# Turns given to other places in a four-layer graph network: block ends behind the third block, and layer 3's small steps

## The chip, the core and the metric

The kernel runs on one core of one Trainium2 chip. A core has five engines that each work through their own list of instructions in order: PE (matrix products), DVE (vector), ACT (scalar functions), POOL (GpSimd) and SP (here: DMA issue). The metric is the device time of one execution in microseconds (us); the kernel before takes 2223.41 us (median of 3 runs, 2222.41 to 2224.99).

## The reference

The input is x (4096 nodes with 128 features) and one sparse adjacency matrix adj (4096 x 4096, kept dense, f32). Four graph layers follow one another, each as `x = layernorm(x + layer(x, adj))`:

```
layer 0:  scores from signs of adj, softmax over edges, h' = (attn * adj) @ (x @ W)
layer 1:  two Chebyshev convolutions (K = 3), each with ELU:
          T1 = adj @ x ; T2 = 2 adj @ T1 - x ; out = x W[0] + T1 W[1] + T2 W[2] + b
layer 2:  4 heads: h = x @ weight.T ; C = src + dst
          tau = adj.T * exp(max(0.2 C, C)) ; z = sum over m of (adj.T * tau / sum tau) h, plus bias
layer 3:  deg = clip(sum adj, 1) ; out = x W_self + (adj @ x / deg) W_neigh
```

The output is x after layer 3.

## The kernel before, in words

The 4096 nodes are 32 tiles of 128 (index `t` or `nt`), and 8 blocks of 512 (`ib` or `b`). The matrix [...] streams in as pieces of 1 MB (`chunk`), again for each product.

**Where the change acts.** Everything from L1035 on is one hand-ordered stretch (`manual_schedule`): on PE, DVE, ACT and POOL the instructions run in the order in which the program emits them. Three kinds of work are woven into one another there:

1. Layer 1's last product (L1118): for each of the eight column blocks, 32 matmuls of w with pieces of the transposed matrix, summed in PSUM. Its accumulator p is emptied by the first instruction of `block_end` (L749).
2. Layer 2's attention. It is done in passes (class `Pass`): passes 0 to 5 are wide (two blocks of 512, two heads each), passes 6 and 7 narrow (one block, four heads). A pass has 32 steps, one for each source tile. In a step DVE makes tau (L880), DVE and POOL multiply it once more with the matrix (L886 to L888; narrow: L892 to L894), and PE sums numerator and denominator over the steps with four matmuls each (L904). ACT copies the piece of the matrix to PSUM (`a`, L852 or L849) and takes the row sums for layer 3's degree along with it.
3. Layer 3's product (`layer3_product`, L991): for each pair of blocks, 64 matmuls of 512 columns, and every column block is then added to acc3 (L998 by ACT for the first pair, L1000 by DVE for the others).

**Places.** Small dependent jobs are Python generators in a queue `chains`. Each `one(chains)` in the main order is a place: it runs the first generator up to its next `yield`. When a generator ends, the next one in the queue starts in the same place. So a `yield` is a gap: whatever stands between two yields is emitted together, and what comes after the yield is emitted behind the matmuls and steps up to the next place. The chains in question:

- `block_end(ib)` (L741): ELU, transposes, residual and layer norm of layer 1's block, transposes of x, then x @ W2S in two halves (L784) and from each half the exponentials cs and es and the weighted features hc (L791 to L796). A step of pass 0 or 1 for a source tile may be emitted only after the block's end is done.
- `block_targets(ib)` (L800): the target side of the scores, dv, one matmul (L804) and a string of copies and subtractions in PSUM (L806 to L813).
- `Pass.targets` (L855): a matmul with selD for each of the pass's four parts and ACT's copy to D.
- `Pass.finish` (L913): transposes of the denominator, reciprocal rd, transposes of the numerator, product z, and POOL adds z to x.
- `layer3_blocks(blocks)` (L937): per block, transposes of x, ACT's copy to xb, four layer-norm statistics on DVE (bn_stats and bn_aggr, lines L142 and L143) and 1/sqrt, then xb @ W3 in two halves (L957), which ACT scales into y and x (L966, L970). Only then `start_product` puts layer 3's product of these blocks into the queue `pieces`.

**How many places there are.** In column blocks 0 to 2 there is a place behind every second matmul (16 per column block). From column block 3 on, a column block is cut into groups by `cuts`: four groups for block 3, six for 4 and 5, five for 6 and 7. Each group has two steps, two places (in its middle and at its end) and then `products()`, PE's sums of earlier steps. Behind layer 1 the loop `while todo` makes rounds of two steps: step, place, step, a further place if no piece of layer 3 is waiting, `products()`, place, and then some layer-3 matmuls: a credit of 2.0 per wide round and 3.4 per narrow round, at most 6, which is set to zero while `pieces` is empty. A round stops handing out matmuls when a column block of layer 3 is complete; its addition to acc3 is emitted after the first step of the next round. What is left when the passes are done is emitted behind them.

Most of the chains' PSUM results go through one pool, ps_x, whose tiles are all named px, with one buffer: a new px waits until the last reader of the one before is done.

Of the kernel before, what the change touches and what calls it, by code (L numbers as in the profile page):

```python
# [33 lines left out]
def adj_resnorm_d4(ctx: ExitStack, tc: tile.TileContext, x_in, xT_in, adj, adjT, w0g, w0gT, a0, w1a, b1a,  # L34
# [10 lines left out]
    NB = N // IB  # L45
# [87 lines left out]
    def transpose4(pool, name, src, order=lambda r: r):  # L133

        p = pool.tile([P, TB, P], F32, name=name)
        for k in range(TB):
            order(nc.tensor.transpose(p[:, k, :], src(k), ident))  # L137
        return p

    def stats(r, t):  # L140
        st = small.tile([P, 6], F32, name="st")
        nc.vector.bn_stats(st, r)  # L142
        nc.vector.bn_aggr(mv[:, t, :], st)  # L143
# [481 lines left out]
    def network(usual):  # L625

        with ExitStack() as whole:
# [113 lines left out]
            def block_end(ib, p):  # L741

                blk = slice(ib * IB, (ib + 1) * IB)
                tb = slice(ib * TB, (ib + 1) * TB)
                pns = []
                oT = l2w.tile([P, IB], F32, name="oT", tag="z")
                rn = l2w.tile([P, 2, IB], F32, name="rn", tag="nd")
                r, n = rn[:, 0, :], rn[:, 1, :]
                nc.vector.tensor_add(oT, p, h0T[:, blk])  # L749
                nc.vector.tensor_scalar(n, oT, B1B, 0.0, op0=ALU.add, op1=ALU.min)  # L750
                nc.scalar.activation(n, n, AF.Exp)
                nc.scalar.activation(r, oT, AF.Relu, bias=B1B)
                nc.vector.scalar_tensor_tensor(oT, n, -1.0, r, op0=ALU.add, op1=ALU.add)
                yield
                if ib <= 2:
                    yield
                q = transpose4(ps_x, "px", lambda k: oT[:, k * P:(k + 1) * P])
                yield
                nc.vector.tensor_add(x[:, tb, :], q, x[:, tb, :])
                for t in range(ib * TB, (ib + 1) * TB):  # L760
                    stats(x[:, t, :], t)
                s = small.tile([P, TB], F32, name="rstd")
                m = small.tile([P, TB], F32, name="mean")
                nc.scalar.activation(s, mv[:, tb, 1], AF.Sqrt, bias=eps)
                nc.vector.reciprocal(s, s)
                nc.vector.scalar_tensor_tensor(m, mv[:, tb, 0], -1.0, s, op0=ALU.mult, op1=ALU.mult)
                for k in range(TB):
                    r = x[:, ib * TB + k, :]
                    nc.scalar.activation(r, r, AF.Identity, bias=m[:, k:k + 1], scale=s[:, k:k + 1])
                yield  # L770
                q = transpose4(ps_x, "px", lambda k: x[:, ib * TB + k, :])
                yield
                nc.scalar.copy(xT[:, blk], q.rearrange("p k i -> p (k i)"))
                nc.scalar.activation(m[:, 0:1], m[:, 0:1], AF.Exp, scale=0.0)
                nc.gpsimd.tensor_tensor(x[:, tb, :], x[:, tb, :], B2R[:, None, :].to_broadcast([P, TB, F]), ALU.add)  # L775
                if ib < NB - 2:
                    yield
                for half in range(2):

                    pool, name = (ps_p, "pp") if ib == NB - 1 and half else (ps_x, "px")  # L780
                    pn = pool.tile([P, 2, F + H], F32, name=name)
                    for k in range(2):
                        t = ib * TB + 2 * half + k
                        nc.tensor.matmul(pn[:, k, :], xT[:, t * P:(t + 1) * P], W2S, start=True, stop=True)  # L784
                    pns.append(pn)
                    if ib == NB - 1 and half == 0:
                        continue
                    yield
                    for pn, at in zip(pns, range(half + 1 - len(pns), half + 1)):
                        two = slice(ib * TB + 2 * at, ib * TB + 2 * at + 2)  # L790
                        nc.scalar.activation(cs[:, two, :], pn[:, :, F:F + H], AF.Exp, scale=0.2)  # L791
                        nc.scalar.activation(es[:, two, :], pn[:, :, F:F + H], AF.Exp, scale=0.8)
                        for k in range(2):
                            t = ib * TB + 2 * at + k
                            nc.vector.tensor_mul(hc[:, t], pn[:, k, 0:F].rearrange("p (h f) -> p h f", f=FO),
                                                 cs[:, t, :][:, :, None].to_broadcast([P, H, FO]))  # L796
                    pns.clear()
                ended.append(ib)

            def block_targets(ib):  # L800

                blk = slice(ib * IB, (ib + 1) * IB)
                pd = ps_x.tile([96, IB], F32, name="px")
                nc.tensor.matmul(pd, WD, xT[:, blk], start=True, stop=True)  # L804
                yield
                nc.scalar.activation(pd, pd, AF.Exp, scale=-0.8)  # L806
                nc.scalar.copy(dv[:, blk], pd)
                yield
                nc.vector.tensor_sub(pd, pd, dv[:, blk])
                nc.scalar.copy(dv[32:64, blk], pd[32:64, :])  # L810
                nc.scalar.copy(dv[64:96, blk], pd[64:96, :])
                nc.vector.tensor_sub(pd[64:96, :], pd[64:96, :], dv[64:96, blk])
                nc.scalar.copy(dv[64:96, blk], pd[64:96, :])  # L813
                if ib < 2:
                    yield
# [4 lines left out]
            class Pass:  # L820
# [92 lines left out]
                def finish(self):  # L913


                    more = (ps_p, "pp") if self in passes[0:2] else (ps_nd, "den") if self is passes[-1] else None
                    turn = lambda pool, name, i: transpose4(pool, name, lambda k: self.nd[:, i, k * P:(k + 1) * P])
                    q = turn(ps_x, "px", 1)
                    if more:
                        qn = turn(*more, 0)  # L920
                    yield
                    rd = small.tile([P, TB, 4], F32, name="rd")
                    nc.vector.reciprocal(rd, q.rearrange("p k (g f) -> p k g f", f=FO)[:, :, :, 0])
                    if not more:
                        qn = turn(ps_x, "px", 0)
                        yield
                    z = l2w.tile([P, TB, 4, FO], F32, name="z")
                    nc.vector.tensor_mul(z.rearrange("p k q f -> p (k q) f"), qn.rearrange("p k (g f) -> p (k g) f", f=FO),
                                         rd.rearrange("p k g -> p (k g)")[:, :, None].to_broadcast([P, TB * 4, FO]))
                    n, f = len(self.blocks), slice(self.heads[0] * FO, (self.heads[-1] + 1) * FO)  # L930
                    for i, b in enumerate(self.blocks):
                        xb = x[:, b * TB:(b + 1) * TB, f].rearrange("p k (h f) -> p k h f", f=FO)
                        eng = nc.vector if self is passes[-1] else nc.gpsimd
                        eng.tensor_tensor(xb, z.rearrange("p k (h b) f -> p k h b f", b=n)[:, :, :, i, :], xb, ALU.add)
                    yield

            def layer3_blocks(blocks):  # L937
# [3 lines left out]
                for j, b in enumerate(blocks):  # L941
# [7 lines left out]
                    nc.scalar.activation(sj, mv[:, b * TB:(b + 1) * TB, 1], AF.Sqrt, bias=eps)  # L949
                    nc.vector.reciprocal(sj, sj)  # L950
                    final = b == NB - 1
                    qs = []
                    for half in range(2):
                        pool, name = ((ps_nd, "den") if final else (ps_p, "pp") if blocks[0] == 0 else (ps_x, "px"))
# [81 lines left out]
            with tc.manual_schedule(engines={mybir.EngineType.PE, mybir.EngineType.DVE, mybir.EngineType.Activation,  # L1036
# [6 lines left out]
                passes = [Pass([2 * mp, 2 * mp + 1], [2 * hp, 2 * hp + 1]) for mp in range(NW - 1) for hp in range(H // 2)]  # L1043
# [33 lines left out]
                def num(this, nt, tau2):  # L1077
                    this.product(False, nt, tau2)
                    if nt == NT - 1 and this is not passes[-1]:
                        if this is passes[0]:  # L1080
                            first_sums.close()
                            ps_a.append(enter(name="ps_a2", bufs=1, space=PSUM))
                        chains.append(this.finish())
                        if this.heads[-1] == H - 1:
                            chains.append(layer3_blocks(this.blocks))
                            chains.append(start_product(this.blocks))
                            if this is passes[1]:
                                chains.append(block_targets(NB - 1))
                        later = passes.index(this) + 2
                        if 2 < later < len(passes):  # L1090
                            chains.append(passes[later].targets())
# [119 lines left out]
```

## Time and profile before

| row of the page | value |
|---|---|
| span | 2221.7 us, 23001 instructions |
| PE busy | 2136.2 us (96%) |
| DVE busy | 1186.1 us (53%) |
| ACT busy | 562.8 us (25%) |
| POOL busy | 857.5 us (39%) |
| L1118, PE, product with w | 203.1 us in the group of pp, 29.1 us in the group of num |
| L904, PE, numerator and denominator | 333.6 us and 339.2 us |
| L991, PE, layer 3's product | 231.7 us |
| L880, DVE, tau | 646.7 us, mean 1059 ns |
| L888, POOL, second factor | 459.4 us, mean 2393 ns |

The profile is that of one execution. Its page divides the span into 40 equal slices and gives each engine's busy share of a slice in tenths. A row of a group names line, engine, operation, output and inputs, then the time that the group was busy, the mean of one instruction and the idle time of the engine just ahead of it, with what ended that idle time. A view of waits sums such idle time by waiting line and by the line that ended it (total, times, longest). A view in order of time gives start, length and instruction, and idle time ahead of it in brackets. An f32 matmul appears there as two records.

### The profile page before, as it was taken

Reading aid. Unit: us, or ns where it says so; the run is one execution under the profiler, and the core shown is the slowest. Engines: PE = TensorE matmul, PEld = TensorE weight load, DVE = VectorE, ACT = ScalarE, POOL = GpSimd, SP = SyncE. Lnnn points to the kernel's source line nnn. Section 1 sums busy time; section 2 is a strip of 40 time slices with the busy share of each in tenths; the row PEclk is TensorE's granted clock in tenths of the full one; section 3 lists DMA queues with packets and bytes.
Section 4 is the critical chain, followed back from the end, with each engine's and each line's share of the span. In section 5 each row is a group of like instructions: output and inputs, shape, how many; then the busy total and the mean of one; then the engine's idle time right before and its main releaser. Section 6 shows DMA issues by size and latency. Waiting matters only on the chain. (4 is left out here: it accounts for less than half of the span.)

```text
span 2221.7 us, 23001 instructions
## 1 busy us (share of the span) xinstructions
PE 2136.2 (96%) x8644; PEld 847.9 (38%) x8644; DVE 1186.1 (53%) x1832; ACT 562.8 (25%) x1014; POOL 857.5 (39%) x539
## 2 busy tenths in 40 slices
PE   8999999999999999999999999979999899999997
PEld 4344454444444444444443333322222222223333
DVE  5655460000011110000016787799999999989995
ACT  6755100000000000000032323235333433232213
POOL 0000000000000000000005676698999899989980
PEclk9999999999999999999999999999999999999999
DMA  9886658888767677777876556525666566635554
GB/s 395 328 324 234 224 201 286 300 302 302 265 229 262 233 240 267 263 263 267 285 256 236 186 195 224 209 79 191 242 230 244 190 243 231 228 132 191 189 174 169
DMA packets 87145, 528.18 MB, mean 238 GB/s; under 512 B 9328, under 2 KB 15472, under 8 KB 25712
## 3 DMA queue, kind: packets, MB, share of 16 engines
q1 hardware_dynamic: 80288, 521.64, 66.6%
q10 hardware_dynamic: 6736, 4.98, 0.7%
q8 instruction: 70, 1.15, 0.2%
q14 instruction: 51, 0.42, 0.1%
HBM read 524.49 MB, written 2.10 MB: 237 GB/s over the span
## 5 line engine op out<-in xcount | busy, mean ns | idle before, releaser
L880 DVE SCALAR_TENSOR_TENSOR tau<-D,es,a 128x1024 f32<-128x1024 f32 (+1 forms) x640 | 646.7, 1059 | 45.9 <-ACT a L852 20.0
L888 POOL TENSOR_TENSOR tau<-tau,chunk 128x1024 f32<-128x1024 f32 x192 | 459.4, 2393 | 13.3 <-DVE tau L880 12.5
L775 POOL TENSOR_TENSOR x<-x,B2R 128x512 f32<-128x512 f32 x8 | 10.2, 1276 | 1145.0 <-PE px L137 1145.0
L904 PE MATMUL num<-tau,hc 128*32 128x512 f32 x2048 | 333.6, 613 | 15.5 <-POOL tau L888 9.1
L904 PE MATMUL den<-tau,cs 128*32 128x512 f32 x2048 | 339.2, 602 | 1.9 <-DVE tau L880 0.4
L991 PE MATMUL pp<-chunk,xT 128*128 128x512 f32 (+1 forms) x488 | 231.7, 604 | 0.0
L852 ACT ACTIVATE a<-chunk 128x1024 f32<-128x1024 f32 x160 | 164.4, 1027 | 253.7 <-DVE tau L886 193.1
L664 PE MATMUL pacc<-chunk,t 128*128 128x512 f32 x512 | 223.5, 592 | 0.0
L664 PE MATMUL pacc<-chunk,v 128*128 128x512 f32 x512 | 222.5, 592 | 0.0
L664 PE MATMUL pacc<-chunk,x 128*128 128x512 f32 x512 | 222.1, 592 | 0.0
L887 POOL TENSOR_TENSOR tau<-tau,chunk 128x320 f32<-128x320 f32 x192 | 168.0, 875 | 127.5 <-DVE tau L880 84.9
L1118 PE MATMUL pp<-chunk,w 128*128 128x512 f32 x448 | 203.1, 598 | 0.8 <-DVE oT L749 0.8
L379 PE MATMUL pacc<-chunk,hw 128*128 128x512 f32 x408 | 187.9, 605 | 0.8 <-DVE hw L421 0.7
L886 DVE TENSOR_TENSOR tau<-tau,a 128x704 f32<-128x704 f32 x186 | 163.4, 879 | 0.0
L894 POOL TENSOR_TENSOR tau<-tau,chunk 128x1024 f32<-128x1024 f32 x64 | 151.8, 2372 | 1.1
L904 PEld LDWEIGHTS num<-tau,hc 128*32 128x32 f32 x2048 | 61.5, 110 | 231.8 <-issue 129.6
L904 PEld LDWEIGHTS den<-tau,cs 128*32 128x32 f32 x2048 | 79.2, 111 | 173.8 <-issue 97.3
L664 PEld LDWEIGHTS pacc<-chunk,v 128*128 128x128 f32 x512 | 97.2, 190 | 122.0 <-issue 122.0
L664 PEld LDWEIGHTS pacc<-chunk,x 128*128 128x128 f32 x512 | 96.3, 190 | 115.8 <-issue 115.8
L664 PEld LDWEIGHTS pacc<-chunk,t 128*128 128x128 f32 x512 | 96.1, 190 | 115.3 <-issue 115.3
L991 PEld LDWEIGHTS pp<-chunk,xT 128*128 128x128 f32 x488 | 85.7, 189 | 128.6 <-issue 125.8
L711 DVE COPY w<-ptr 128x512 f32<-128x512 f32 x8 | 5.5, 692 | 241.5 <-PE ptr L137 241.5
(243 smaller groups left out, 1688.4 us busy)
## 6 DMA issues: line engine op xcount, KB each, us to landing
chunk<-in_adjT SPq DMA_DIRECT2D x386, 1024.0 KB, 4.9
chunk<-in_adj SPq DMA_DIRECT2D x80, 1024.0 KB, 5.0
chunk<-in_adj SPq DMA_DIRECT2D x32, 512.0 KB, 4.7
keep<-in_adjT SPq DMA_DIRECT2D x13, 1024.0 KB, 11.4
xT<-in_xT ACTq DMA_DIRECT2D x8, 256.0 KB, 6.6
out<-o ACTq DMA_DIRECT2D x7, 256.0 KB, 2.3
W1A<-in_w1a ACTq DMA_DIRECT2D x1, 384.0 KB, 6.8
W1B<-in_w1b ACTq DMA_DIRECT2D x1, 384.0 KB, 7.5
```

Of the source, the lines that this page charges most:

```text
L379: in_order(nc.tensor.matmul(p, hw[:, j * TB + k, :], a[:, k, :], start=first and k == 0, stop=last and k == TB - 1))
L664: nc.tensor.matmul(p, stationary(c * TB + k), a[:, k, :], start=n == 0 and k == 0, stop=n == NB - 1 and k == TB - 1)
L775: nc.gpsimd.tensor_tensor(x[:, tb, :], x[:, tb, :], B2R[:, None, :].to_broadcast([P, TB, F]), ALU.add)
L852: nc.scalar.activation(ap, a, AF.Copy, accum_out=deg[:, nt, self.mp:self.mp + 1])
L880: nc.vector.scalar_tensor_tensor(flat(tau[:, q:q + n]), flat(self.D[:, q:q + n]), es[:, nt, head:head + 1], ap, op0=ALU.max, op1=ALU.mult)
L886: nc.vector.tensor_tensor(t2[:, 0:OWN], t[:, 0:OWN], (a if only else ap)[:, 0:OWN], ALU.mult)
L887: nc.gpsimd.tensor_tensor(t2[:, OWN:WB], t[:, OWN:WB], a[:, OWN:WB], ALU.mult)
L888: nc.gpsimd.tensor_tensor(t2[:, WB:2 * WB], t[:, WB:2 * WB], a, ALU.mult)
L894: nc.gpsimd.tensor_tensor(tau2[:, 2:4, :], tau[:, 2:4, :], rep(a, 2), ALU.mult)
L904: nc.tensor.matmul(acc[32 * q:32 * q + 32, :], weights(nt, head, is_den), r[:, q, :], start=nt == 0, stop=nt == NT - 1)
L991: nc.tensor.matmul(p, y[:, c * TB + k, :], a[:, k, lo:lo + n], start=c == blocks[0] and k == 0, stop=end)
L1118: nc.tensor.matmul(p, w[:, c * TB + k, :], a[:, k, :], start=c == 0 and k == 0, stop=c == NB - 1 and k == TB - 1)
```

## The change

Six edits, all of them yields. Nothing else differs; every engine does the same work, in partly other order.

- `block_end`, block 2: one place less ahead of its first transposes, and one less between the copy of xT and x @ W2S.
- `block_end`, blocks 3 and 4: a place between the first half of W2S (its exponentials and hc) and the second.
- `block_targets`, blocks 3 to 6: a place between the block's end and the targets' matmul.
- `finish`, passes 2 to 6: a place between the pass's last products and its transposes.
- `layer3_blocks`, all blocks but the last: a place between the copy of x and the statistics on one side and the products with W3 on the other.

The purpose is that the producer of a transpose or a product is further ahead of it in the queue, and that each block's end and targets lie within the column block that follows.

```diff
-                if ib <= 2:
+                if ib < 2:
                     yield
                 q = transpose4(ps_x, "px", lambda k: oT[:, k * P:(k + 1) * P])
...
-                if ib < NB - 2:
+                if ib < NB - 2 and ib != 2:
                     yield
                 for half in range(2):
 
                     pool, name = (ps_p, "pp") if ib == NB - 1 and half else (ps_x, "px")
+                    if half and ib in (3, 4):
+                        yield
                     pn = pool.tile([P, 2, F + H], F32, name=name)
...
             def block_targets(ib):
 
                 blk = slice(ib * IB, (ib + 1) * IB)
+                if 2 < ib < NB - 1:
+                    yield
                 pd = ps_x.tile([96, IB], F32, name="px")
...
+                    if self in passes[2:-1]:
+                        yield
                     q = turn(ps_x, "px", 1)
...
                     final = b == NB - 1
+                    if not final:
+                        yield
                     qs = []
```

## The prediction

> **What bounds the kernel now.** I read the page first, then who waited for whom on PE, then the order of time of one wait after another, and last the starts of DVE's L880, which mark the rounds. The change begins to act after 1170 us, in the product with w (L1118), so the page is read from slice 22 on.
>
> ```profile
> PE   8999999999999999999999999979999899999997
> DVE  5655460000011110000016787799999999989995
> POOL 0000000000000000000005676698999899989980
> ```
>
> Slices are 55.5 us. From 1170 to 1440 us PE is full while DVE and POOL have room: PE sets the pace. From 1500 us DVE and POOL are full as well. There PE's nines deceive: a wide round (two steps) starts every 6.36 us, and its 16 accumulating matmul groups (4 x 0.86 us) and two L991 matmuls (0.89 us each) need 5.2 us. DVE needs 2 x 3.18 us (L880 starts at 1551.9, 1555.2 and so on), POOL 2 x (0.87 + 2.37) less overlap. So wide rounds are bound by DVE and POOL. Narrow rounds take 6.60 us with DVE, POOL and PE close together.
>
> ```profile
> PE px L137 <- ACT dv L813: 5.4, 1, 5.4
> PE px L957 <- ACT xb L945: 4.3, 4, 2.2
> PE px L804 <- DVE hc L795: 0.9, 1, 0.9
> ```
>
> These are PE's waits that the edits touch (total, times, longest). Only the first and third lie in the stage that PE bounds. The first, in order of time on PE:
>
> ```profile
> 1216.93 3.70 PE L1118 MATMUL pp<-chunk,w 128*128 128x512 f32 x8
> 1226.02 1.12 PE L137 MATMUL px<-ident,oT 128*128 128x128 f32 x4 [5.39 <-ACT dv L813]
> 1227.07 1.94 PE L904 MATMUL num<-tau,hc 128*32 128x512 f32 x8
> ```
>
> Block 3's transposes share a place with the last part of block 2's targets: px has one buffer, and PE stands until ACT's last copy out of it (L813). What that costs is read from the spacing of L749 on DVE, once per column block:
>
> ```profile
> 1212.61 0.69 DVE L749 TENSOR_TENSOR oT<-pp,xT 128x512 f32<-128x512 f32 x1 [2.67 <-PE pp L1118]
> 1273.57 0.69 DVE L749 TENSOR_TENSOR oT<-pp,xT 128x512 f32<-128x512 f32 x1 [1.63 <-PE pp L1118]
> 1330.89 0.69 DVE L749 TENSOR_TENSOR oT<-pp,xT 128x512 f32<-128x512 f32 x1
> ```
>
> Column blocks 4 and 5 hold the same matmuls and the same six groups: 60.96 and 57.32 us. In the second PE waits 0.65 us for the normalized x (L769), 0.60 for POOL and 0.32 for hc.
>
> In the layer-3 part I take the round of blocks 2 and 3 (DVE, idle time in brackets):
>
> ```profile
> 1727.11 0.26 DVE L142 BATCH_NORM_STATS2 st<-x 128x6 f32<-128x128 f32 x1
> 1727.41 0.18 DVE L143 BATCH_NORM_AGGREGATE mv<-st 128x2 f32<-128x6 f32 x1
> 1730.12 0.18 DVE L950 RECIPROCAL rstd<-rstd 128x4 f32<-128x4 f32 x1 [2.53 <-ACT rstd L949]
> 1730.21 2.44 DVE L880 SCALAR_TENSOR_TENSOR tau<-D,es,a 128x1024 f32<-128x1024 f32 x2
> ```
>
> DVE stands 2.53 us because ACT's square root is queued behind the copy of xb, an `a` load and the copy of a finished layer-3 column block (L998 at 1726.37). The whole cost of a boundary is its rounds' excess over 6.36 us: 4.29 and 3.15 here (10.65 and 9.51 us).
>
> **What the skill says.** Trainium Architecture — The Big Picture, "Inside one NeuronCore": every engine has its own stream, and they meet only at semaphores. The trace agrees: the 5.39 us are PE's, while DVE went on until its own queue needed PE. PSUM — Partial Sum Buffer, "Specifications (TRN2)": 8 banks of 2 KiB per partition; a px of 512 f32 is one whole bank, which fits the single buffer seen in the waits. ScalarE: Activation LUTs, "What ACT_TABLE_LOAD costs": 1283 ns for the load; the trace has 1.28 us, at 1728.49, inside the 2.53 us. TensorE: Matmul & The Clock Gate, Part 1, says that idleness slows the array; here the accumulating group right after the 5.39 us took 1.94 us against 1.06 usually, so a little more than the wait itself may come back.
>
> **Layer 1's last product.** I counted the places by the code. Two edits take one place each from block 2. Its end and targets then fill exactly the 8 places of column block 3 instead of running 2 places into column block 4. Block 3's transposes get the first place there, as block 4's have in column block 5. So column block 4 should look like column block 5: 60.96 - 57.32 = 3.64 us saved, the new waits of 0.65 and 0.60 included. The second W2S half of blocks 3 and 4 gets its own place, which removes the 0.32 us wait for hc. The target matmul of block 6 (L804) gets its own place too: 0.88. Sum: **-4.8 us**. New placing costs nothing elsewhere: block 2's transposes come after four L1118 matmuls (3.55 us) while oT is ready 2.5 us after the stage starts; its x transposes come after a group of products (2.6) and four more matmuls, as block 6's have now without a wait; copying xT and the first W2S half share a place, again as in block 6. Target copies of blocks 4 to 6 go one to two places later, still within places that are empty now. The waiting engine would be PE, with L1118 behind it. Bounds: -6.6 (5.39 + 0.32 + 0.88, nothing new) to -3.0 (block 2 also gets block 4's 1.25, and a little more).
>
> **Blocks 0 and 1 of layer 3.** The same DVE work, two statistics of some 2.2 us (1.6 plus 0.36 of ACT plus 0.18), now falls in two rounds instead of one; the sum is the same. PE loses its 0.74 and 2.96 us waits, which PE's slack hides. Copying out block 7's targets and the first selD share a place as before, but after products: PE can wait some 3.3 us there against 2.11 now, and arrive later at the next column block's end. **+0.5**, bounds -1.3 to +1.5.
>
> **Blocks 2 and 3.** The statistics no longer stand in the round that begins with the L998 copy ahead of them, but at its end. That round: 6.36 + 1.04 (what L998 costs in an ordinary round: 7.40 us) + 2.25 = 9.65; the next 6.36; the third 8.6. Sum 24.6 against 10.65 + 9.51 + 6.37 = 26.5: **-1.9**, bounds -2.5 to 0. The extra place ahead of the `finish` transposes moves rd and z by half a round; the wait of 0.65 us there is PE's and hidden.
>
> **Blocks 4 and 5.** Rounds 70 to 74 now exceed 6.60 us by 9.44 in sum. After: two accumulations of 0.6 and perhaps 0.4 of waiting, rd and z 0.8, statistics 4.5, one late `a` load 1.2: 7.9. That is -1.5, and I take 0.5 more because PE's backlog delays the next accumulation (2.0 us of DVE wait at 1986) a little less: **-2.0**, bounds -3.5 to 0.
>
> **The end.** Each layer-3 product starts only after its blocks' chain. By my count blocks 2, 3 and blocks 4, 5 start one round later, and four L991 matmuls, one more column block of block 6, remain when the last step is done: 12 instead of 8.
>
> ```profile
> 2162.93 3.70 PE L991 MATMUL pp<-chunk,xT 128*128 128x512 f32 x8
> 2166.56 1.07 PE L904 MATMUL num<-tau,hc 128*32 128x512 f32 x8
> 2161.98 2.35 POOL L894 TENSOR_TENSOR tau<-tau,chunk 128x1024 f32<-128x1024 f32 x1
> ```
>
> Four of them now stand before the last num group, though POOL's result is there at 2164.33. With one matmul there instead, num starts some 2.0 us earlier and the last round lacks an accumulation (0.6). Later, where PE has no gaps until 2207, four matmuls are added: 4 x 0.89 = 3.56. **+0.9**, bounds +0.3 to +4.2 (nothing saved before num, and one accumulation more).
>
> Sum: -4.8 + 0.5 - 1.9 - 2.0 + 0.9 = **-7.3 us**, so 2223.4 - 7.3 = 2216.1 us.
>
> **The rivals.** (A) No change: the layer-1 stage gains its 4.8, but the later statistics are only displaced, and the spilled product costs its full price: -4.8 + 0.5 + 4.2 = -0.1, 2223.3 us. For it: DVE and POOL are full there, so smoothing waits of PE buys nothing. Against it: the 2.53 us are DVE's own. (B) Slower: block 3's wait returns as waits for x in blocks 2 and 3, because their normalization now stands ahead of an `a` load in ACT's queue (DVE waited 2.82 us for `a` in block 4), leaving -1.0; each of three boundaries loses 1.5 to waits on px between places with no products between them; the end +4.2: +7.7, 2231.1 us. For it: such neighbouring places exist (selD behind the scaling copies). Against it: DVE has 20% room in the first stage. (C) All waits vanish, every favourable bound but the end's: -6.6 - 1.3 - 2.5 - 3.5 + 0.9 = -13.0, 2210.4 us.
>
> **How the numbers follow.** Forecast 0.60, A 0.20, B 0.08, C 0.12. The range from 2211.5 to 2221.5 holds the forecast's spread and leaves out half of C, most of A and B. Faster by over 0.2% means below 2219.0: the forecast but for 0.04 of its upper edge, and C: 0.68. Within: that edge and most of A: 0.22. Slower: B and a little of A: 0.10.
>
> **What would show it.** The 5.39 us before L137 on oT gone, and 57 us between block 3's and block 4's L749; the span up to block 7's L749 shorter by 4 to 5 us. No 2.53 us before L950. Rounds of blocks 2 and 3 summing to under 25 us. Eight more L991 records (four matmuls) after the last num group, which starts right behind POOL's last L894. The prediction is wrong if column block 3 grows by more than a microsecond (a wait for oT or x), if DVE waits for `a` at the moved statistics, or if the end grows by over 3 us.

## The result and the profile after

The changed kernel takes 2214.03 us (median of 4 runs, 2212.91 to 2215.16) against 2223.4 us (4 runs): ratio 0.9957, 95% interval 0.994 to 0.9974. That is 9.4 us less; 7.3 were forecast. The profiled span goes from 2221.7 to 2213.3 us.

From the page of the changed kernel, the rows of the 40 slices:

```profile
PE   8999999999999999999999999979999899989997
DVE  5655460000010110000026877899999999999995
POOL 0000000000000000000004766698999999999980
```

The pattern is as before, a few us earlier: no other engine has become the bound, and what changed is inside the slices. Inserted lines shift the numbers: L880 is now L884, L886 is L890, L894 is L898, L904 is L908, L950 is L956, L991 is L999, L998 is L1006, L1118 is L1126; L749 stays.

PE in order of time, where it stood for 5.39 us before:

```profile
1217.80 1.99 PE L1126 MATMUL pp<-chunk,w 128*128 128x512 f32 x4
1219.62 0.60 PE L137 MATMUL px<-ident,oT 128*128 128x128 f32 x4
1220.06 1.88 PE L1126 MATMUL pp<-chunk,w 128*128 128x512 f32 x4
...
1228.07 1.48 PE L137 MATMUL px<-ident,x 128*128 128x128 f32 x4 [0.64 <-ACT x L769]
```

Block 3's transposes of oT follow at once; only the wait for the normalized x is there, 0.64 us, as in column block 5 before. DVE's starts of L749 for blocks 3, 4 and 5:

```profile
1214.34 0.69 DVE L749 TENSOR_TENSOR oT<-pp,xT 128x512 f32<-128x512 f32 x1 [2.23 <-PE pp L1126]
1271.09 0.69 DVE L749 TENSOR_TENSOR oT<-pp,xT 128x512 f32<-128x512 f32 x1 [0.59 <-PE pp L1126]
1327.99 0.69 DVE L749 TENSOR_TENSOR oT<-pp,xT 128x512 f32<-128x512 f32 x1 [0.59 <-PE pp L1126]
```

Column block 4 took 60.96 us and takes 56.75; column block 5 took 57.32 and takes 56.89. The clock that PE was granted there changed too. In these rows it is the third figure from the end (1.00 is the full clock); first before, then after:

```profile
1212.60:1273.60 61.00, 55.61 (x280) 20.24 (x282) 46.79 (x59) 19.33 (x37) 39.67 (x25) 0.94 0.52 189
1214.30:1271.10 56.80, 55.40 (x279) 19.48 (x282) 45.34 (x57) 16.59 (x32) 38.61 (x25) 1.00 0.57 206
```

DVE in order of time at the statistics of block 2 in layer 3:

```profile
1726.21 0.26 DVE L142 BATCH_NORM_STATS2 st<-x 128x6 f32<-128x128 f32 x1
1726.51 0.18 DVE L143 BATCH_NORM_AGGREGATE mv<-st 128x2 f32<-128x6 f32 x1
1727.06 0.18 DVE L956 RECIPROCAL rstd<-rstd 128x4 f32<-128x4 f32 x1 [0.36 <-ACT rstd L955]
1727.15 2.44 DVE L884 SCALAR_TENSOR_TENSOR tau<-D,es,a 128x1024 f32<-128x1024 f32 x2
```

2.53 us of waiting have become 0.36. ACT, in order of time, shows why:

```profile
1720.09 0.59 ACT L1006 COPY acc<-pp 128x512 f32<-128x512 f32 x1 [4.86 <-PE pp L999]
1720.57 1.03 ACT L856 ACTIVATE a<-chunk 128x1024 f32<-128x1024 f32 x1
...
1722.66 0.57 ACT L951 COPY xb<-px 128x512 f32<-128x512 f32 x1
1723.25 1.28 ACT L955 ACT_TABLE_LOAD   x1
1726.73 0.30 ACT L955 ACTIVATE rstd<-mv,eps 128x4 f32<-128x4 f32 x1 [2.20 <-DVE mv L143]
```

The copy of the layer-3 column block, the copy of xb and the table load are all over at 1724.5, before DVE has finished the statistics. Now ACT waits for DVE, and not DVE for ACT. PE at the end:

```profile
2153.23 1.12 PE L999 MATMUL pp<-chunk,xT 128*128 128x512 f32 x2
2154.29 1.57 PE L908 MATMUL num<-tau,hc 128*32 128x512 f32 x8
...
2164.51 3.70 PE L999 MATMUL pp<-chunk,xT 128*128 128x512 f32 x8
...
2168.99 3.70 PE L999 MATMUL pp<-chunk,xT 128*128 128x512 f32 x8
...
2173.48 3.70 PE L999 MATMUL pp<-chunk,xT 128*128 128x512 f32 x8
```

As forecast: one product matmul (two records) stands ahead of the last numerator instead of four, and three groups of four follow it later where there were two. In the whole trace 96 records of the product stand behind it instead of 88.

**Where the time went.** The starts of tau on DVE divide what follows layer 1's last product into 102 rounds of two steps, counted from 0. Lengths in us, from the trace of one execution each; "layer 1" is an edit of `block_end` and `block_targets`, "finish" and "blocks" are the place in `finish` and in `layer3_blocks` alone:

| stretch | before | after | layer 1 alone | finish alone | blocks alone | finish and blocks |
|---|---|---|---|---|---|---|
| column block 3 (block 2's end in it) | 41.85 | 43.03 | 43.02 | 41.84 | 41.83 | 41.84 |
| column block 4 | 60.96 | 56.75 | 56.76 | 61.94 | 61.21 | 60.67 |
| column blocks 5 to 7 | 158.07 | 156.23 | 156.23 | 158.04 | 158.05 | 158.04 |
| block 7's L749 to round 0 | 3.63 | 4.44 | 4.44 | 3.63 | 3.63 | 3.64 |
| round 13 (blocks 0, 1) | 8.66 | 8.11 | 8.66 | 9.82 | 7.40 | 7.39 |
| rounds 22 to 25 | 28.04 | 27.15 | 28.04 | 27.16 | 28.04 | 27.15 |
| rounds 38 to 44 (blocks 2, 3) | 52.66 | 50.37 | 52.62 | 52.83 | 52.43 | 50.37 |
| rounds 70 to 75 (blocks 4, 5) | 49.04 | 47.09 | 49.04 | 47.14 | 49.40 | 47.09 |
| rounds 76 to 78 | 22.49 | 19.79 | 20.39 | 23.01 | 21.92 | 19.79 |
| rounds 79 to 100 | 164.81 | 167.48 | 165.04 | 164.35 | 164.77 | 167.62 |
| round 101 to the end | 66.39 | 67.26 | 66.45 | 66.43 | 66.42 | 67.43 |

Rounds left out differ by 0.1 us or less, but for 0.45 more in rounds 45 to 69 of "blocks alone". From block 2's L749 to the end it is 1050.92 us before and 1041.99 after: 8.93 less.

**What goes with the clock.** Each run lists the mean share of its full clock that PE was granted: 0.987 to 0.990 in the 85 executions of the kernel before that the later runs list, 0.991 or 0.992 in the four of the changed kernel. Among those 85 the time falls by 1.1 us for each 0.001 of clock. By that figure some 3 of the 9.4 us go together with a higher clock. This is an estimate: slow stretches follow waits of PE, so it overlaps with the waits that the change removes. The time at half clock is therefore given below wherever a stretch depends on it.

### The profile page after: what moved, and what is told of

Its sections match the earlier page's. It is cut to its first block, busy times and chain, and to the rows that moved or that the text cites. A ratio compares the mean times of both kernels' runs of the same rounds, so it can differ in the third digit from the quotient of the medians.

```text
span 2213.3 us, 22997 instructions
## 1 busy us (share of the span) xinstructions
PE 2139.9 (97%) x8644; PEld 850.8 (38%) x8644; DVE 1186.3 (54%) x1832; ACT 562.4 (25%) x1014; POOL 857.6 (39%) x539
## 5 line engine op out<-in xcount | busy, mean ns | idle before, releaser
L884 DVE SCALAR_TENSOR_TENSOR tau<-D,es,a 128x1024 f32<-128x1024 f32 (+1 forms) x640 | 646.4, 1058 | 44.0 <-ACT a L856 24.8
L908 PE MATMUL num<-tau,hc 128*32 128x512 f32 x2048 | 333.9, 606 | 15.0 <-POOL tau L892 9.0
L908 PE MATMUL den<-tau,cs 128*32 128x512 f32 x2048 | 343.6, 597 | 3.3 <-DVE tau L884 0.8
L999 PE MATMUL pp<-chunk,xT 128*128 128x512 f32 (+1 forms) x488 | 232.9, 607 | 0.0
L1126 PE MATMUL pp<-chunk,w 128*128 128x512 f32 x448 | 204.3, 598 | 0.8 <-DVE oT L749 0.8
L890 DVE TENSOR_TENSOR tau<-tau,a 128x704 f32<-128x704 f32 x186 | 163.1, 877 | 0.0
L898 POOL TENSOR_TENSOR tau<-tau,chunk 128x1024 f32<-128x1024 f32 x64 | 151.8, 2372 | 1.0
L908 PEld LDWEIGHTS num<-tau,hc 128*32 128x32 f32 x2048 | 62.4, 109 | 230.9 <-issue 127.8
L908 PEld LDWEIGHTS den<-tau,cs 128*32 128x32 f32 x2048 | 80.4, 110 | 177.0 <-issue 86.9
L999 PEld LDWEIGHTS pp<-chunk,xT 128*128 128x128 f32 x488 | 85.8, 190 | 133.1 <-issue 130.5
```

Source lines behind the costliest of these rows:

```text
L884: nc.vector.scalar_tensor_tensor(flat(tau[:, q:q + n]), flat(self.D[:, q:q + n]), es[:, nt, head:head + 1], ap, op0=ALU.max, op1=ALU.mult)
L890: nc.vector.tensor_tensor(t2[:, 0:OWN], t[:, 0:OWN], (a if only else ap)[:, 0:OWN], ALU.mult)
L898: nc.gpsimd.tensor_tensor(tau2[:, 2:4, :], tau[:, 2:4, :], rep(a, 2), ALU.mult)
L908: nc.tensor.matmul(acc[32 * q:32 * q + 32, :], weights(nt, head, is_den), r[:, q, :], start=nt == 0, stop=nt == NT - 1)
L999: nc.tensor.matmul(p, y[:, c * TB + k, :], a[:, k, lo:lo + n], start=c == blocks[0] and k == 0, stop=end)
L1126: nc.tensor.matmul(p, w[:, c * TB + k, :], a[:, k, :], start=c == 0 and k == 0, stop=c == NB - 1 and k == TB - 1)
```

## The experiments

All kernels were timed in five rounds beside the kernel before on the same chip: it took 2224.16 us (median) beside e1 to e4, 2224.52 beside e5 to e8 and 2223.83 beside e9 to e12. These are three chips, so kernels of different groups are compared best by their ratios.

**The layer-1 edits alone, and the layer-3 edits alone.** Do the two halves add up?

```diff
 e1:  block_end, block_targets as changed; finish, layer3_blocks as before
 e2:  finish, layer3_blocks as changed; block_end, block_targets as before
```

> Only the edits of block_end and block_targets, layer 3 as before. Theory (two separate gains that add up): the stage of layer 1's last product is 4.0 us shorter (start of the first round behind it, as in the changed kernel, after taking off the 0.5 us by which that trace starts later), and everything behind it is only shifted: 2219.4 us, 4.0 under the kernel before. Rival (the stage's gain is absorbed by the rounds behind it, which DVE and POOL bound, and the whole gain comes from the layer-3 edits): 2222.5 to 2223.4 us.

> Only the edits of finish and layer3_blocks, layer 1 as before. Theory: -0.6 at the first boundary, -0.9 in the round with selD and the copy L998, -2.3 for blocks 2 and 3, -2.0 for blocks 4 and 5 and +0.9 at the end, sum -4.9: 2218.5 us. Rival (most of the gain is layer 1's, DVE's 2.53 us only move): 2221 to 2223.4 us.

Measured: layer 1 alone 2219.28 us, ratio 0.9979 (0.9971 to 0.9987); layer 3 alone 2217.89 us, 0.9972 (0.9961 to 0.9983). The product of the ratios is 0.9951, within the changed kernel's interval, so no interaction of the halves is seen within the noise. The layer-3 half is worth 6.3 us in its series (its interval is 3.8 to 8.7) where the prediction's terms for it add up to 2.5; layer 1 is worth 4.9 (2.9 to 6.4). Which half is the larger isn't shown, as the intervals overlap. In the table each half repeats the changed kernel's numbers in its own part and nearly those of before in the other, but for round 13 and rounds 76 to 78 (see below).

**The two layer-3 places apart.**

```diff
 e3 (finish alone)
+                    if self in passes[2:-1]:
+                        yield
                     q = turn(ps_x, "px", 1)
 e4 (layer3_blocks alone)
+                    if not final:
+                        yield
                     qs = []
```

> Only the place ahead of the transposes in finish. By count no layer-3 product starts a round later and 8 matmuls are left at the end, as before. Theory: the selD matmuls of the pass after next fall half a round later, one less of them stands ahead of the L991 matmuls that the copy L998 waits for, and round 25 loses 0.9 us: 2222.5 us. Rival: the 0.65 to 2.3 us waits of PE for rd (6.0 us in sum) count for the time: 2217 to 2220 us.

> Only the place in layer3_blocks between the copy with the statistics and the products with W3. By count the products of blocks 2, 3 and 4, 5 start in the same rounds as before and 8 matmuls are left at the end. Theory: DVE no longer waits behind ACT's copy, -0.6, -2.3 and -1.9 us in the rounds of the three pairs, nothing at the end: 2218.6 us. Rival (this edit pays only together with the one in finish): no more than -2 us, 2221.4 us or above.

Measured: finish alone 2221.64 us, 0.9986 (0.9979 to 0.9992); blocks alone 2220.35 us, 0.9983 (0.9975 to 0.9991). The product of the two ratios is 0.9969, and both together have 0.9972: in the whole time the two places simply add up.

Finish alone gains 2.5 us, more than its theory's 0.9. Its trace has the 0.9 in rounds 22 to 25, and 1.9 more in rounds 70 to 75, where the theory expected nothing.

For blocks alone the time decides nothing: -3.8 us lies between theory (-4.8) and rival (-2), and the theory's ratio is inside the interval. The trace speaks against the theory's mechanism: DVE's wait at the statistics is still there, to the hundredth. But this trace is of the slowest of the kernel's 14 executions (2223.01 us) and shows only 1.1 us less than before from block 2's L749 on. Where the usual execution gains the rest is not shown. Thirteen of the 14 were granted a clock of 0.990 or more; at 1.1 us for each 0.001 that would account for some 3 us, an estimate.

```profile
1726.90 0.18 DVE L143 BATCH_NORM_AGGREGATE mv<-st 128x2 f32<-128x6 f32 x1
1729.61 0.18 DVE L950 RECIPROCAL rstd<-rstd 128x4 f32<-128x4 f32 x1 [2.53 <-ACT rstd L949]
```

With finish alone that wait is gone (0.36 us), but two rounds later DVE stands elsewhere. DVE, and then ACT, in order of time:

```profile
1746.70 0.88 DVE L886 TENSOR_TENSOR tau<-tau,a 128x704 f32<-128x704 f32 x1
1749.95 2.47 DVE L880 SCALAR_TENSOR_TENSOR tau<-D,es,a 128x1024 f32<-128x1024 f32 x2 [2.37 <-POOL tau L888]
```

```profile
1745.32 0.37 ACT L968 ACTIVATE xT<-px,rstd 128x128 f32<-128x128 f32 x1 [3.26 <-PE px L959]
...
1748.69 1.04 ACT L852 ACTIVATE a<-chunk 128x1024 f32<-128x1024 f32 x1
```

ACT's scaling (L968) waits 3.26 us for PE's product with W3 (L959), emitted in the same place as the statistics; the `a` load that DVE needs is queued behind it and starts only at 1748.69. The trace names POOL as the releaser, but DVE starts at 1749.95, when ACT's `a` (1748.69 + 1.04) is just done. In the traces with both places this wait is gone. The rounds 39 to 43:

```
                    39     40     41     42     43    sum
before            7.05   6.36  10.65   9.51   6.37  39.94
blocks alone      7.04   6.36  10.65   8.50   7.15  39.70
finish alone      6.53   6.87   9.40   8.49   8.80  40.09
both, and after   6.53   6.87   9.40   6.34   8.49  37.63
```

In these traces neither place alone gains more than 0.3 us here, and together they gain 2.3. But how much of ACT's 3.26 us is the order's own is not shown, because in the trace of finish alone PE ran at half its clock from 1736.4 to 1743.2, just ahead of that W3 product:

```profile
1738.06 1.94 PE L904 MATMUL num<-tau,hc 128*32 128x512 f32 x8
1739.76 1.94 PE L904 MATMUL den<-tau,cs 128*32 128x512 f32 x8
1741.47 1.89 PE L904 MATMUL num<-tau,hc 128*32 128x512 f32 x8
```

The three groups start 1.71 us apart instead of 0.86, so the product comes some 2.6 us later than at full clock. Without that, `a` would be done at about 1747.2, before DVE is ready for it at 1747.6, and finish alone would have about 37.7 us, as both have (an estimate from these lines). What is shown is that both together are safe: the seven traces with both and no empty places have 37.6 us, with half clock in these rounds (finish and blocks, 6.8 us from 1731.0) or without (the changed kernel).

Rounds 70 to 79 don't behave likewise: 78.12 us before, 77.92 with blocks alone, 76.75 with finish alone, 76.05 with both. (Round 79 belongs to them: a wait that stands in round 78 before stands in 79 with both.) There the place in `finish` brings most by itself.

**Block 2's two places given back** to the changed kernel.

```diff
-                if ib < 2:
+                if ib <= 2:
                     yield
...
-                if ib < NB - 2 and ib != 2:
+                if ib < NB - 2:
                     yield
```

> The changed kernel with the two places of block 2 put back. Theory: block 2's end and targets again reach two places into the next column block, block 3's transposes again stand some 5 us behind ACT's last copy out of px; column block 4 takes 61 us again instead of 56.8 and column block 3 loses its 1.2 us: +3.0 us against the changed kernel, about 2217.0 us or 6.5 under the kernel before. Rival (the places of blocks 3 to 6 alone bring layer 1's gain, and block 2's edits only cost the 1.2 us): -1 us against the changed kernel, 10.5 under the kernel before.

Measured: 2216.76 us, 0.9964 (0.9951 to 0.9978). The old wait is back on PE, and column block 4 takes 61.47 us:

```profile
1216.43 3.70 PE L1126 MATMUL pp<-chunk,w 128*128 128x512 f32 x8
1225.51 1.11 PE L137 MATMUL px<-ident,oT 128*128 128x128 f32 x4 [5.38 <-ACT dv L817]
```

From block 2's L749 to the end it needs 2.5 us more than the changed kernel; the medians differ by 2.7, near the theory's 3.0. The intervals of the two ratios overlap, so it is the traces that carry this. The saving in column block 4 (4.7) isn't all kept: column block 3 gives 1.2 back, and the rest is lost later.

**The narrow rounds' credit.** Does the spilled product cost what it seems? Kernel e6 is the changed kernel with the credit raised; e10 and e11 are the kernel before with the credit raised and lowered. By count 8, 4 and 12 matmuls are then left behind the last step (12 in the changed kernel, 8 before), and no product starts in another round. The records behind the last numerator agree: 88, 80 and 96 (96 in the changed kernel, 88 before).

```diff
-  credit = min(credit + (2.0 if todo and todo[0][0].wide else 3.4), 6.0) if pieces else 0.0
+  credit = min(credit + (2.0 if todo and todo[0][0].wide else 3.5), 6.0) if pieces else 0.0
   (e6, e10; in e11 3.2)
```

> The changed kernel with a credit of 3.5 instead of 3.4 in narrow rounds. By count 8 instead of 12 layer-3 matmuls are left at the end, as in the kernel before; no other place moves. Theory (the end costs 0.9, as its two traces show, since the last num group now starts right behind POOL): the stretch behind the last round falls from 67.3 back to 66.4 us, and an accumulation of 0.6 comes back into the rounds: -0.3 to -0.9 us against the changed kernel. Rival (the four matmuls cost their full 3.56 us): -3 us or more.

> The kernel before with one number changed: the credit of a narrow round is 3.5 layer-3 matmuls instead of 3.4. By count the products start in the same rounds as before, and 4 matmuls are left behind the last step instead of 8. Theory: the narrower credit's gain in the changed kernel (2.7 us) belongs to the narrow rounds and not to the change, so the kernel before gains as much: 2220.7 us, ratio 0.9988. Rival: it depends on where the column blocks' ends fall in the changed order; then the kernel before gains only what four matmuls fewer at the end are worth, 0 to 0.9 us: 2222.5 to 2223.4.

> The kernel before with the credit of a narrow round at 3.2 instead of 3.4: the start of every product stays where it was, and 12 matmuls instead of 8 are left behind the last step, as in the changed kernel. It measures the end's term alone. Theory (the sum of the prediction): the stretch from the last round to the end grows by 0.9 us, since one column block no longer stands ahead of the last numerator, and the rounds before it keep their length within 0.5: 2224.3, ratio 1.0004. Rival: the spilled column block costs its full price, 4.2 us at the end: 2227.6, ratio 1.0019.

Measured: e6 2211.42 us (2211.2 to 2211.98), 0.994 (0.9926 to 0.9954); e10 2224.58 us, 1.0003 (0.9995 to 1.0011); e11 2224.9 us, 1.0002 (0.9994 to 1.001). The last is the end's term by itself: four matmuls more behind the last step lengthen the stretch from round 101 on from 66.39 to 67.50 us, 1.1 and not 4.2, because the last numerator no longer has four product matmuls ahead of it. Rounds 79 to 100 give 0.56 of it back. The rival of 2227.6 us (1.0019) lies outside the interval. In the trace of e10 the four matmuls fewer shorten the end by 3.15 us (to 63.24), but rounds 79 to 100, which take them in, grow by 2.51. There four matmuls still stand ahead of the last numerator, so nothing hides the end's price, and the rounds take it back. The gain of e6, 2.6 us against the changed kernel, is not a gain of the number 3.5: the kernel before has none from it. That is more than was expected of e6, and near the rival's 3 us, though not by the rival's way. Its trace puts 2.3 us into rounds 85 to 100, where three rounds instead of four take the 8.1 us of a round that PE fills with its groups and four product matmuls, and 0.4 at the end. Why the column blocks end more favourably there was not traced further.

**The products later still**: the changed kernel with five empty places ahead of the x transposes of blocks 2, 3 and of blocks 4, 5.

```diff
+                if blocks[0] in (2, 4):
+                    for _ in range(5):
+                        yield
                 s = small.tile([P, 2 * TB], F32, name="rstd2")
```

> The changed kernel with five empty places more ahead of the transposes of blocks 2, 3 and of blocks 4, 5; no instruction is added. By count the products of these pairs start one and two rounds later and 16 instead of 12 matmuls are left at the end. Theory: the slack ahead of the last num group was used up by the first four, so these cost nearly in full: 3.56 less one accumulation of 0.6, +3.0 us against the changed kernel, the stretch behind the last round 70 to 71 us. Rival (what is left at the end stays hidden): +1 us at most.

Measured: 2218.82 us, 0.9975 (0.9965 to 0.9984): 4.8 us slower, more than expected. Rounds 70 to 100 get 5.8 us shorter, since less of layer 3 lies in them, but the end grows from 67.26 to 76.46. PE there:

```profile
2149.14 3.70 PE L1002 MATMUL pp<-chunk,xT 128*128 128x512 f32 x8
2152.77 1.07 PE L908 MATMUL num<-tau,hc 128*32 128x512 f32 x8
...
2162.50 3.70 PE L1002 MATMUL pp<-chunk,xT 128*128 128x512 f32 x8 [1.55 <-DVE acc L1011]
```

Four matmuls stand ahead of the last numerator again, four more than in the changed kernel remain, and PE runs into a wait for the accumulator. What the rounds save, the end takes with interest.

**Other places in layer 1's part**: the second W2S half also at block 5, the targets' place only at blocks 3 and 4; once with the credit of 3.5 and once, beside the changed kernel, with 3.4.

```diff
-                    if half and ib in (3, 4):
+                    if half and ib in (3, 4, 5):
                         yield
...
-                if 2 < ib < NB - 1:
+                if ib in (3, 4):
                     yield
```

> A version that may beat both: the changed kernel with block 5 among the blocks whose two W2S halves have a place between them, with the place ahead of the targets for blocks 3 and 4 alone, and with the credit of 3.5. Theory: block 5's wait for hc goes (1.1 us), block 7's vector work no longer stands behind block 6's target copies (0.8 us), block 6's target matmul waits 0.9 us for hc again, and the credit gives 0.3 to 0.9: -1.4 us against the changed kernel. Rival: these waits are not on the path, within 0.5 us of the changed kernel.

> The changed kernel with the places of the second W2S half at blocks 3, 4 and 5 and of the targets at blocks 3 and 4 alone, and the credit as it was (3.4). Theory: the places of blocks 5 and 6 are worth nothing, since the waits only move, so 2214.0 within 0.5, equal to the changed kernel on the same chip. Rival: they are worth the 0.7 to 1.5 us of waits that they take away: 2212.5 to 2213.3.

> The changed kernel once more, beside the three others on the same chip, as their measure: 2214.0 us, ratio 0.9957.

Measured: with 3.5 2211.55 us, 0.9943 (0.993 to 0.9957), no better than e6; with 3.4 2213.97 us, 0.9956 (0.9942 to 0.997), and the changed kernel beside it 2214.1 us, 0.9952 (0.9939 to 0.9966). The places are worth nothing. A new wait takes the place of those removed:

```profile
1362.85 1.88 PE L1126 MATMUL pp<-chunk,w 128*128 128x512 f32 x4
1365.87 1.07 PE L808 MATMUL px<-xT,WD 128*96 128x512 f32 x2 [1.14 <-DVE hc L797]
```

From block 2's L749 to round 0 that kernel takes 260.63 us, the changed one 260.45. The fastest kernel of all is thus the changed one with a credit of 3.5.

## Why the prediction was right, point by point

In short: the two waits that the prediction named are gone, and the spilled product costs what it said. That the total came within 2.1 us is partly luck, since errors of both signs stand in it: column block 3 and block 7 cost 2.0 us that were put at nothing, one edit brought 0.9 us that was put at nothing, and round 13 gave 1.1 us more than forecast, while its length moves by more than that with PE's clock.

**Layer 1's last product (-4.8): right mechanism, -4.06 measured** (264.51 to 260.45 us). Column block 4 gained 4.21 where 3.64 were expected. The wait of 5.39 us cost more than itself, as the prediction guessed: PE ran at half its clock from 1222.96 to 1229.79, and the transposes and the two groups behind the wait took 1.12, 1.94 and 1.54 us where 0.60, 1.06 and 1.04 are usual. All seven traces with block 2's old places have 3.4 or 6.8 us of half clock in this column block and take 60.53 to 61.94 us; the seven with the new ones have none and take 56.74 to 56.77. Two costs were missing. First, "placing costs nothing elsewhere" failed: column block 3 grew by 1.18 us, past the microsecond that the prediction named as a sign against it. PE waits at block 2's second W2S half, which has no place of its own:

```profile
1195.80 1.88 PE L1126 MATMUL pp<-chunk,w 128*128 128x512 f32 x4
1198.69 0.69 PE L786 MATMUL px<-W2S,xT 128*128 128x132 f32 x4 [1.01 <-DVE hc L797]
```

1.01 of the 1.18 us stand in that line. The hc it waits for is late: DVE ahead of it waited for an `a` load that ACT had queued behind block 2's normalization, rival B's mechanism.

```profile
1184.23 0.16 DVE L766 SCALAR_TENSOR_TENSOR mean<-mv,rstd 128x4 f32<-128x4 f32 x1
1187.15 2.47 DVE L884 SCALAR_TENSOR_TENSOR tau<-D,es,a 128x1024 f32<-128x1024 f32 x2 [2.76 <-ACT a L856]
```

DVE's slack took 2.76 us with little harm; PE's wait is the part that counts. Second, block 7's transposes wait 0.71 us for oT (at 1431.41): 0.81 us more between its L749 and round 0. DVE's L750 takes 1.31 us there instead of 0.49, as POOL has 1.03 us of its work on tau left when L750 starts. With the targets' place at blocks 3 and 4 alone (e8, e9) that stretch takes 3.63 us again, but column blocks 5 to 7 take 1.0 more.

**Blocks 0 and 1 (+0.5): not decided.** Rounds 8 to 13 show -0.6, nearly all of it in round 13. Over all 14 traces the length of that round goes with the time that PE spent at half clock in the 17 us ahead of it:

```
half clock ahead   length of round 13 (us)
none               7.39 finish and blocks, 7.40 blocks alone, 7.40 e9
3.4 us             8.66 before, layer 1 alone and e11
                   7.80 to 8.17 changed kernel (twice), e5, e6, e7, e8
6.8 us             9.82 finish alone, 9.80 e10
```

That moves the length by 2.4 us, far more than the 0.6 in question. With the same 3.4 us the kernels without the layer-3 edits take 0.5 to 0.9 us longer, so the sign leans against the prediction. But there the slow stretch also lies 1 to 4 us further ahead of the round, and no kernel without these edits was traced with no slow stretch, so the order's own share stays open.

**Rounds 22 to 25: a gain that was not foreseen, -0.9.** The prediction gave the place in `finish` no price. "Finish alone" has the gain (27.16 us), "blocks alone" has not (28.04). DVE is idle for 0.94 us ahead of a tau in round 25 (at 1615.36) instead of 1.83 (at 1620.32): the `a` load that it needs is queued on ACT behind a copy of a layer-3 column block, and this copy now comes sooner after DVE's own work. Which of PE's small waits and matmuls ahead of it makes the difference was not separated.

**Blocks 2 and 3 (-1.9): right size, wrong owner.** The three rounds gave 9.40 + 6.34 + 8.49 = 24.23 us, forecast 24.6; -2.3 with the rest. But the prediction put the place in `finish` at nothing and so left it to `layer3_blocks` to move the statistics to the far side of the copy of the finished column block. The place in `finish` does that, by moving the whole chain half a round: alone it takes the 2.53 us away, and blocks alone does not. The one in `layer3_blocks` keeps ACT from standing at PE's W3 afterwards; that it is needed at full clock too is not shown. The clock is not what makes the 2.3 us: both kernels with the two places have 37.6 us in rounds 39 to 43, one with 6.8 us of half clock there and one with none.

**Blocks 4 and 5 (-2.0): -1.98 over rounds 70 to 100**, later starts of the products included, though one execution can't carry that number. (The prediction's own terms for the rounds after, 1.2 + 0.4 + 0.8 + 4.5 + 1.2, add up to 8.1 and not 7.9, which gives -1.8; and the step that it has start at 1551.9 starts at 1552.04.) Kernels with the order of before in this part have 22.49 (before) and 20.39 us (layer 1 alone) in rounds 76 to 78, at the same instructions in the same order. The windows show what differs, PE's granted clock (the figure ahead of the DMA share). Before:

```profile
1960.00:1965.00 5.00, 1.55 (x9) 0.77 (x5) 3.76 (x7) 3.75 (x13) 1.97 (x3) 0.86 0.00 0
1965.00:1970.00 5.00, 5.00 (x25) 1.19 (x28) 5.00 (x9) 1.49 (x5) 5.00 (x4) 0.50 0.01 3
```

and layer 1 alone, which is there 4.8 us earlier:

```profile
1950.00:1955.00 5.00, 4.33 (x21) 1.53 (x24) 4.68 (x13) 0.73 (x2) 5.00 (x3) 0.66 0.55 201
1955.00:1960.00 5.00, 3.19 (x25) 1.13 (x17) 3.57 (x7) 3.75 (x14) 1.95 (x3) 1.00 0.00 0
1960.00:1965.00 5.00, 5.00 (x37) 1.79 (x37) 5.00 (x8) 2.45 (x7) 5.00 (x3) 1.00 0.01 3
```

In the first, PE waits 2.22 and 1.23 us for ACT's scaling and then runs at half its clock for 6.8 us (1963.65 to 1970.48), with DVE behind it. In the second the slow stretch falls ahead of that wait, which shrinks from 2.22 to 0.58 us: the same slowness, hidden. So the term rests on which execution it is set against: -1.98 against before, -0.1 against layer 1 alone. The trace of the changed kernel has 6.8 us of half clock there as that of before has (from 1959.5; its long round is then 79, 9.01 us), while that of layer 1 alone is of its second quickest execution of 15 (2216.97 us, median 2219.28). So the first is the like comparison. Firm in it are rounds 70 to 75: 49.04 us in the four kernels with the old order there, 46.98 to 47.11 in the seven with both layer-3 edits and no empty places. Finish alone has 47.14 and blocks alone 49.40, so this part is the place in `finish` by itself.

**The end (+0.9): +0.87**, and shown separately by e11.

Sum of the stretches: -4.1 - 0.6 - 0.9 - 2.3 - 2.0 + 0.9 = -9.0, and 8.93 in the whole. Against the forecast's -7.3 blocks 0 and 1 gave 1.1 more, the place in `finish` 0.9, blocks 2 and 3 0.4, and layer 1 0.7 less. The first of these can't be credited to the order, as that round's length follows the clock.

Rival A (no change) fell: the statistics weren't only displaced, and the spill didn't cost 4.2. Rival B's mechanism exists but costs PE 1.0 us, not 8. Rival C's 2210.4 us was out of reach for this change.

## What to carry to other kernels

A place inserted into a dependent chain acts on every later link: before pricing an edit, follow on each engine's queue what its shift puts ahead of what, because the edit that looked idle (`finish`) moved the statistics past the copy, and the one that looked decisive did not. Test two small edits in all four combinations, and read the granted clock of each trace beside them: here a stretch seemed to need both, while one of the four traces ran that stretch at half clock, and over the whole time the two simply added up. A wait on the engine that sets the pace is worth removing only while no neighbour that shares its buffer or its producer takes it over; read this from the spacing of a recurring instruction, not from the sum of waits.

## What the runs showed of the hardware

That PE's half clock decides 2.1 us of rounds 76 to 78 between two kernels of the same order, and 2.4 us of round 13, was not expected. The Trainium skill, "TensorE: Matmul & The Clock Gate", Part 1, says that an idle window of some 3.4 us halves the clock, and that the window runs freely, so that the number of slow matmuls varies from run to run. The traces agree with the half (0.50 granted; groups at a spacing of 1.71 us instead of 0.86) and with the variation. The length is shown too: in each of the 14 traces every stretch at half clock but the last, which runs to the end, is 3.41 or 6.83 us long, and their starts lie whole multiples of 3.41 us apart. But PE need not be idle for a whole window, and what counts is where its waits fall in this grid. The same two waits stand in before and in layer 1 alone:

```profile
1954.13 0.66 PE L137 MATMUL px<-ident,x 128*128 128x128 f32 x4 [1.23 <-ACT x L970]
1955.46 1.13 PE L957 MATMUL px<-W,xb 128*128 128x256 f32 x4 [0.68 <-ACT xb L945]
```

```profile
1949.35 0.66 PE L137 MATMUL px<-ident,x 128*128 128x128 f32 x4 [1.23 <-ACT x L974]
1950.68 1.61 PE L961 MATMUL px<-W,xb 128*128 128x256 f32 x4 [0.68 <-ACT xb L949]
```

In before the slow stretch from 1963.65 puts a window at 1953.41 to 1956.82. It holds 0.72 + 0.68 = 1.4 us of these waits, and PE keeps its full clock behind it. In layer 1 alone the slow stretch starts at 1951.18. The window ahead of it begins at 1947.77 and holds both waits, 1.9 us.

Divided by this grid, the 14 traces have 4181 windows at full clock between 1150 and 2195 us. In 4088 of them PE was idle for less than 1.7 us, and none of these is followed by half clock. In 63 it was idle for more than 2.0 us, and all of these are. Of the 30 between, 14 are. So in this program idle time of about half a window is enough, whether in one wait or in several, and the page's idle window is too strict. (PE's ends are modelled in the trace, so the idle times are estimates.)

DVE's L750, a TENSOR_SCALAR of 128x512, takes 0.49 us when POOL is idle. When a tau instruction of POOL overlaps its start, it ends some 0.3 us after POOL's end: with 1.03, 0.82, 0.34 and 0.11 us of POOL's work left it took 1.31 us (block 7, after), 1.10 (block 7, e5), 0.62 (block 4, after) and 0.49 (block 7, e9). This price, here up to 0.8 us, depends on where POOL stands, and no sum of waits shows it.
